# The end of the last item: second norm in two parts, a stretch without gathers, b2's products one half step later

## The chip, the cores and the metric

The kernel runs on one core of one Trainium2 chip. The metric is the device time of one execution in microseconds (us); times given for a kernel are medians over several runs, with the lowest and the highest run beside them. Engine names are those of the profile: PE is TensorE (matrix products and transposes), PEld its weight loads, DVE is VectorE, ACT is ScalarE, POOL is GpSimd, SP is the engine that issues most DMAs.

## The reference, cut to what matters

The input x is (8, 256, 32, 32) in float32: eight items, each of 1024 tokens with 256 channels. Two layers follow one another.

```
# layer 0: attention of 8 heads of 64, the softmax over the query axis, w_out, residual
a[i, j] = softmax over i of (q[i] . k[j] / 8), for each head
x[i] = x[i] + (sum over j of a[i, j] v[j], heads side by side) @ w_out + b_out

# layer 1, on t (1024 tokens x 256 channels of an item)
n1 = norm(t);  t = t + softmax(n1 W^T n1^T) n1
n2 = norm(t);  t = t + moe(n2)

def moe(n2):                              # 8 experts, each token takes its best two
    rw, re = top2(softmax(n2 @ router_w.T));  rw = rw / sum(rw)
    out = n2
    for e in range(8):
        out += gate[:, e] * (gelu(n2 @ w1[e] + b1[e]) @ w2[e] + b2[e])
    return out
```

Here norm takes the mean off each token and divides by the root of its variance plus 1e-5, and gate[:, e] is the token's weight for expert e, zero where e is not among its two. At the end t goes back to the channel-first form of x.

## The kernel before, in words

**Tiling.** Tokens lie in eight blocks of 128 (NT = 8, P = 128 partitions), channels in two halves of 128 (NCC = 2); a "half step" of the dense experts works on 512 tokens (NH2 = 2 halves) of one expert (E = 8).

**Stages.** Items 0 to 7 go one after another through layer 0 and through the attention of layer 1 (`attend`). For items 0 to 6 the second norm (`normed`), the router (`logits`, `gates`) and `dispatch` follow; `dispatch` scatters each token's normed row twice, to the rows of its two experts in DRAM, and t + n2 is stored to DRAM (`sums`). Once item 7 is through layer 0, `experts` computes the expert products on those scattered rows and leaves the results in DRAM (`y`). What then remains of items 0 to 6 is to fetch for each token its two result rows, multiply them by the gates and add them: that is class `Results`. It is spread over the last stage, which is item 7's own `attend` and `dense`.

**Results.** There are 56 units, one for each block of items 0 to 6. A unit is *sent* by two indirect DMAs on POOL (`gather`, tile yk, line L1108), into one of 8 slots, and *added* by two DVE instructions (`add`, o, L1130). When the eight units of an item are added, its two halves are *stored* (`store`): one DVE transpose (oT, L1164) and four DMAs of 128 KB on SP's queue (L1170). `tick(place, behind)` hangs these on places of item 7's work; the table PLACES says for each place how many units are added, sent and stored. The additions are issued behind the instruction `behind`; the gathers get an order dependency on it. A scheduler orders the instructions of each engine, but keeps to these dependencies and to `issue_after`.

**Item 7's end, in its order.**

- *The last mixing.* `mix(7)` transposes the probabilities (pa, L672), copies them (aT, L674) and multiplies them with n1 (py, L679, 8 products of 128x256 for a block). DVE's "mixed" instruction (t, L684) divides by the sum of the softmax and adds t. The hook `fill("last products")` stands between aT and py of block 7.
- *The norm.* `layer_norm` takes bn_stats and bn_aggr of all eight blocks (L227 on), then adds eps, takes the root on ACT, the reciprocal on DVE (L231), and writes n2 by one DVE instruction for each block (n, L233). The tile n2 uses the buffer tag "n", the same as n1, so n2's first write waits until py of block 7 has read n1.
- *To channels.* `to_channels` makes 16 transposes on PE (pt_n, L243) and two DVE copies of 128x1024 (n2T, L244), one for each half of the channels.
- *The sum.* POOL adds n2 to t (L794), one instruction of 128x2048.
- *The router.* Eight router products (pl, L706) lead to a copy on ACT (lT, L714), two transposes (plT), DVE's copy g_l (L732), the maximum, a subtraction, exp on ACT (g_p), and some twenty small DVE instructions until all_gates (L1201 to L1203).
- *The dense experts.* `dense` makes 16 half steps. `hidden` makes eight products 128x512 (pdh, L1227) and two gelu on ACT (dh, L1236); `collect` makes 16 products 128x256 (pdy, L1251) and four DVE instructions that add gate times pdy to t (L1260). The program goes `hidden(k + 1)`, `collect(k)`. Three experts' weights have a buffer each; when expert e is done, SP loads those of expert e + 3 (`weights`, L1177 and L1181).
- *The biases.* gate times b2, summed over the experts, is one more product: `biases` transposes all_gates (pg, L1209, eight times), copies them on ACT (gT, L1211), makes 16 products with b2 (pb, L1215) and has DVE add them to t (L1218). It is called between hidden(1) and collect(0):

```
for at, (e, n) in enumerate((e, n) for e in range(E) for n in range(NH2)):
    now = (e, n, hidden(e, n))
    if at == 1:
        biases()
    if pending is not None:
        collect(*pending)
    pending = now
```

After the last expert, item 7's two halves go out by the same `store`.

Of the kernel before, what the change touches and what calls it, by code (L numbers as in the profile page):

```python
# [10 lines left out]
F32 = mybir.dt.float32  # L11
I32 = mybir.dt.int32
AF = mybir.ActivationFunctionType
ALU = mybir.AluOpType
# [5 lines left out]
def kernel(  # L20
# [23 lines left out]
    nc = tc.nc  # L44
    P = 128
    B, C, S = x.shape
    E, D, FF = w1.shape
# [4 lines left out]
    NT = S // P  # L52
# [12 lines left out]
    one = ctx.enter_context(tc.tile_pool(name="one", bufs=1))  # L65
# [3 lines left out]
    small = ctx.enter_context(tc.tile_pool(name="small", bufs=6))  # L69
# [147 lines left out]
    def bcast(t, n):  # L217

        return t.unsqueeze(2).to_broadcast([P, NT, n])

    def layer_norm(t, dst, eps, name):

        mv = small.tile([P, NT, 2], F32, tag="mv", name=f"mv_{name}")
        for i in range(NT):
            st = small.tile([P, nc.vector.BN_STATS_DIM], F32, tag="st", name=f"st_{name}_{i}")
            nc.vector.bn_stats(st, t[:, i, :])
            nc.vector.bn_aggr(mv[:, i, :], st)  # L227
        rstd = small.tile([P, NT], F32, tag="rstd", name=f"rstd_{name}")
        nc.vector.tensor_scalar_add(rstd, mv[:, :, 1], eps)
        nc.scalar.activation(rstd, rstd, AF.Sqrt)  # L230
        nc.vector.reciprocal(rstd, rstd)  # L231
        for i in range(NT):
            written = nc.vector.tensor_scalar(  # L233
                dst[:, i, :], t[:, i, :], mv[:, i, 0:1], rstd[:, i : i + 1], ALU.subtract, ALU.mult
            )
        return written

    def to_channels(t, dst, name):

# [107 lines left out]
    class Begin:  # L347
# [3 lines left out]
        def __init__(self, b, xT):  # L351
            self.b, self.xT = b, xT
            self.v = None
            self.qks = [[]]
            self.todo = list(range(NT))
# [270 lines left out]
    def attend(b, t1, fill, tick=nothing):  # L626
        n1 = one.tile([P, NT, D], F32, tag="n", name=f"n1_{b}")
        layer_norm(t1, n1, 1e-5, f"a{b}")
        fill("norm 1")
        nT = one.tile([P, NCC, S], F32, tag="nT", name=f"nT_{b}")  # L630
        to_channels(n1, nT, f"n1_{b}")
        fill("normed 1")
        xa = one.tile([P, NCC, S], F32, tag="xa", name=f"xa_{b}")
        for ec in range(NCC):
            px = big(f"px_{b}_{ec}")
            for dc in range(NCC):
                for n in range(NH2):
                    nc.tensor.matmul(  # L638
                        px[:, ts(n, 512)],
                        WT[:, dc, ts(ec, P)],  # L640
                        nT[:, dc, ts(n, 512)],
                        start=(dc == 0),
                        stop=(dc == NCC - 1),
                    )
            tick(("xa", ec), nc.vector.tensor_copy(xa[:, ec, :], px))

        t2 = t1

        def scores(i):
            psc = big(f"ps1_{b}_{i}")  # L650
            for ec in range(NCC):
                for n in range(NH2):
                    nc.tensor.matmul(  # L653
                        psc[:, ts(n, 512)],
                        xa[:, ec, ts(i, P)],
                        nT[:, ec, ts(n, 512)],
                        start=(ec == 0),
                        stop=(ec == NCC - 1),
                    )
            nmax = small.tile([P, 1], F32, tag="nmax", name=f"nmax_{b}_{i}")  # L660
            tick(("max", i), nc.vector.tensor_reduce(nmax, psc, AX.X, ALU.max, negate=True))  # L661
            ex = expp.tile([P, 1024], F32, tag="exps", name=f"ex1_{b}_{i}")
            ssum = small.tile([P, 1], F32, tag="ssum", name=f"ssum_{b}_{i}")
            nc.scalar.activation(ex, psc, AF.Exp, bias=nmax, scale=1.0, accum_out=ssum)  # L664
            return ex, ssum

        def mix(i, ex, ssum):
            if i == NT - 1:
                fill("last weights")
            pt = big(f"pa_{b}_{i}")  # L670
            for m in range(NT):
                nc.tensor.transpose(pt[:, ts(m, P)], ex[:, ts(m, P)], ident)  # L672
            aT = two.tile([P, S], F32, tag="tr", name=f"aT_{b}_{i}")
            nc.vector.tensor_copy(aT, pt)  # L674
            if i == NT - 1:
                fill("last products")
            py = acc(f"py_{b}_{i}")
            for m in range(NT):
                nc.tensor.matmul(  # L679
                    py[:, :D], aT[:, ts(m, P)], n1[:, m, :], start=(m == 0), stop=(m == NT - 1)  # L680
                )
            rs = small.tile([P, 1], F32, tag="rs1", name=f"rs1_{b}_{i}")
            nc.vector.reciprocal(rs, ssum)
            mixed = nc.vector.scalar_tensor_tensor(  # L684
                t2[:, i, :], py[:, :D], rs, t1[:, i, :], ALU.mult, ALU.add
            )
            tick(("mixed", i), mixed)

        pending = None
        for i in range(NT):  # L690
            now = (i, *scores(i))
            if pending is not None:
                mix(*pending)
            pending = now
        mix(*pending)
        return t2

# [85 lines left out]

    groups = [Group(n, items) for n, items in enumerate(GROUPS)]

    def normed(b, t2, fill, tick=nothing):

        n2 = one.tile([P, NT, D], F32, tag="n", name=f"n2_{b}")
        tick("normed", layer_norm(t2, n2, 1e-5, f"f{b}"))
        fill("norm 2")  # L790
        nT = one.tile([P, NCC, S], F32, tag="nT", name=f"n2T_{b}")
        tick("turned", to_channels(n2, nT, f"n2_{b}"))

        nc.gpsimd.tensor_add(t2, t2, n2)  # L794
        fill("normed 2")
        l = logits(b, nT)
        return n2, nT, l
# [256 lines left out]
    class Results:  # L1054
# [9 lines left out]
            **{("max", i): (0, 1, 0) for i in range(1, 8)},  # L1064
            ("mixed", 0): (4, 2, 0),
            **{("mixed", i): (3, 2, 1 if i > 2 else 0) for i in range(1, 7)},
            ("mixed", 7): (0, 2, 0),
            "normed": (0, 2, 0),
            "turned": (3, 2, 0),
            "gates": (3, 2, 0),  # L1070
            ("dense", 0): (3, 2, 2),
            ("dense", 1): (3, 2, 0),
            **{("dense", k): (2, 2, 2) for k in range(2, 16)},
        }

        def __init__(self, group):
# [71 lines left out]
        def tick(self, place, behind=None):  # L1148
            added, sent, stored = self.PLACES.get(place, (0, 0, 0))
            if added:  # L1150
                with tc.issue_after(behind.ins):
                    for _ in range(added):
                        self.add()
            for _ in range(sent):
                self.gather(behind)
            for _ in range(stored):
                if self.whole:
                    b, total, n = self.whole.pop(0)
                    store(b, total, n)

    def store(b, total, n):

        oT = two.tile([P, D // SQ, P], F32, tag="qk1", name=f"oT_{b}_{n}")
        nc.vector.transpose(  # L1164
            oT.rearrange("p g (t i) -> p i g t", i=NB),
            total[:, ts(n, NB), :].rearrange("p i (g c) -> p i g c", c=SQ),
        )
        dst = out[b].rearrange("(g c) (n a k) -> n a c g k", c=SQ, n=NH2, a=NQ)
        for a in range(NQ):
            nc.sync.dma_start(dst[n, a], oT[ts(a, SQ)])  # L1170

    def dense(b, t2, tick):


        def weights(e):
# [11 lines left out]
        nc.sync.dma_start(b2_rows, b2)  # L1187
        for e in range(NWB):
            weights(e)
        _, nT, l = normed(b, t2, tick, tick)  # L1190
        routing = gates(b, l)
        while True:
            try:
# [80 lines left out]
        pending = None  # L1274
        for at, (e, n) in enumerate((e, n) for e in range(E) for n in range(NH2)):
            now = (e, n, hidden(e, n))
            if at == 1:
                biases()
            if pending is not None:
                collect(*pending)  # L1280
            pending = now
# [7 lines left out]
    for b in range(B):  # L1289
        xT = next_x  # L1290
        if b + 1 < B:
            next_x = load_x(b + 1)
        if b > 0:
            xs = load_squares(b)
        t1 = layer0(b, xT, begun, routing, xs)
        if b + 1 < B:
            begun = Begin(b + 1, next_x)
            t2 = attend(b, t1, begun.at)
            n2, _, l = normed(b, t2, begun.at)
            nc.sync.dma_start(groups[0].sums[b], t2)  # L1300
            routing = dispatch(b, n2, l, groups[0])
            continue
        experts(groups[0])
        others = Results(groups[0])
        others.begin()
        t2 = attend(b, t1, others.tick, others.tick)
        dense(b, t2, others.tick)
        assert others.added == len(others.units) and not others.whole


# [40 lines left out]
```

## Time and profile before

| what | value |
|---|---|
| time, median of 3 runs | 2412.4 us (2410.83 to 2414.67) |
| the profiled execution, its own time | 2419.8 us |
| its span in the profile | 2418.1 us |
| granted TensorE clock, mean of the span | 0.993 |
| busy: PE, PEld, DVE, ACT, POOL | 98%, 54%, 64%, 39%, 17% of the span |
| PE's last product ends | 2409.94 us |
| last store lands | 2416.79 us |
| item 7's last mixing product ends | 2272.20 us |
| item 7's all_gates are written | 2296.86 us |

The profile is of one execution, which took longer than the median of the runs; durations and positions below come from it. "Busy" counts the time in which an engine works on an instruction. A line of the timeline gives the start from the beginning of the span in us, the length from the first to the last instruction of the line in us, the engine, the source line, the operation, the output and the inputs with their shapes, the number of instructions, and in brackets the idle time ahead of it and what ended that. "remote" stands for an event that the profile does not put down to an instruction.

### The profile page before, as it was taken

The page shows a single profiled execution, that of the slowest core. Times are in us where ns is not written, and L with a number is a line of the kernel's source. Part 1 is how long each engine was busy: PE and PEld are TensorE (multiplying, and loading weights), DVE is VectorE, ACT ScalarE, POOL GpSimd, SP SyncE. Part 2 cuts the span into 40 slices and gives each one's busy share as a digit, 9 for nine tenths or more (in the row PEclk, how much of TensorE's full clock was granted, in tenths as well). Part 3 has the DMA queues.
Part 4 walks back from the last instruction along what each step waited for, and adds up shares of the span by engine and source line. Part 5 has one row for each costly group of instructions (what it writes and reads, how often), then busy time and mean ns, then how long its engine had stood idle before and what let it go on. Part 6 is the DMA issues. An engine that isn't in the chain of part 4 may idle for free.

```text
span 2418.1 us, 36817 instructions
## 1 busy us (share of the span) xinstructions
PE 2363.3 (98%) x13759; PEld 1315.7 (54%) x13759; DVE 1546.1 (64%) x3658; ACT 939.3 (39%) x1570; POOL 419.0 (17%) x391
## 2 busy tenths in 40 slices
PE   9999999999999999999999999999998999999798
PEld 3356534654466346633663366435643488886565
DVE  5774587567845785578547864786478753335865
ACT  3651366126612662166215631564145522221211
POOL 0000011001200020002000300030002144444652
PEclk9999999999999999999999999999999999999899
DMA  8993201010101010101000100000001166664553
GB/s 297 385 385 93 53 19 36 1 36 15 40 1 35 10 45 1 35 5 49 1 18 18 51 3 18 18 30 8 10 26 52 46 204 219 209 218 150 163 147 101
DMA packets 114778, 196.59 MB, mean 81 GB/s; under 512 B 15752, under 2 KB 58408, under 8 KB 112808
## 3 DMA queue, kind: packets, MB, share of 16 engines
q1 hardware_dynamic: 89592, 127.05, 16.0%
q0 software_dynamic: 25008, 67.20, 8.9%
q8 instruction: 109, 1.79, 0.3%
q14 instruction: 69, 0.57, 0.1%
HBM read 108.88 MB, written 110.90 MB: 91 GB/s over the span
## 4 chain that ended last, share of the span: by engine, by line
PE 91%; DVE 5%; ACT 2%; issue 1%; another core or an unknown queue 1%; DMA 1%; SPq 0%; DVEq 0%; ACTq 0%; POOLq 0%
PE po L528 19%; PE psc L451 18%; PE py L679 9%; PE ps L653 8%; PE pqk L333 7%; PE pr L619 5%; PE ph L1000 4%; PE pe L1025 4%; PE pv L370 4%; PE px L638 2%; PE pdy L1251 2%; PE pa L672 2%; PE pdh L1227 2%; PE pqk L311 2%; PE px L990 1%
## 5 line engine op out<-in xcount | busy, mean ns | idle before, releaser
L492 ACT ACTIVATE ex<-psc,nmax 128x1024 f32<-128x1024 f32 x512 | 570.5, 1115 | 312.3 <-DVE scrap L475 228.2
L451 PE MATMUL psc<-qk,qk 64*64 64x512 f32 x4096 | 576.6, 594 | 10.3 <-ACT ex L492 10.3
L528 PE MATMUL po<-ex,vs 64*64 64x512 f32 x4096 | 571.8, 592 | 1.5 <-DVE vs L508 0.5
L475 DVE TENSOR_SCALAR_CACHE_REDUCE scrap<-psc,nmax 128x512 f32<-128x512 f32 x512 | 384.5, 751 | 151.6 <-PE psc L451 124.6
L466 DVE TENSOR_REDUCE nmax<-psc 128x1 f32<-128x512 f32 x512 | 350.7, 685 | 9.3 <-PE psc L451 9.3
L451 PEld LDWEIGHTS psc<-qk,qk 64*64 64x64 f32 x4096 | 179.9, 132 | 287.1 <-ACT ex L492 138.9
L528 PEld LDWEIGHTS po<-ex,vs 64*64 64x64 f32 x4096 | 175.8, 132 | 275.3 <-issue 82.2
L679 PE MATMUL py<-n,aT 128*128 128x256 f32 x1024 | 239.6, 388 | 6.3 <-DVE aT L674 3.7
L653 PE MATMUL ps<-nT,xa 128*128 128x512 f32 x512 | 236.0, 592 | 0.0
L679 PEld LDWEIGHTS py<-n,aT 128*128 128x128 f32 x1024 | 192.9, 192 | 70.5 <-DVE aT L674 42.2
L863 POOL DMA_INDIRECT rows<-n,d_at x112 | 109.2, 975 | 661.7 <-DVE nmax L466 661.4
L664 ACT ACTIVATE ex<-ps,nmax 128x1024 f32<-128x1024 f32 x64 | 71.3, 1115 | 353.1 <-DVE nmax L661 320.5
L794 POOL TENSOR_TENSOR t<-t,n 128x2048 f32<-128x2048 f32 x8 | 36.2, 4531 | 919.2 <-DVE n L233 919.2
L333 PE MATMUL pqk<-xT,wqkv 128*128 128x512 f32 x384 | 171.2, 599 | 0.0
L684 DVE SCALAR_TENSOR_TENSOR t<-py,rs,t 128x256 f32<-128x256 f32 x64 | 30.8, 482 | 198.9 <-PE py L679 195.1
L653 PEld LDWEIGHTS ps<-nT,xa 128*128 128x128 f32 x512 | 93.5, 190 | 81.2 <-issue 75.1
L333 PEld LDWEIGHTS pqk<-xT,wqkv 128*128 128x128 f32 x384 | 71.0, 190 | 99.9 <-issue 77.8
L1108 POOL DMA_INDIRECT yk<-y,yat x112 | 108.9, 972 | 92.7 <-DVE t L1260 30.0
L619 PEld LDWEIGHTS pr<-wo,res 128*128 128x128 f32 x512 | 120.7, 331 | 3.7 <-ACT res L546 3.7
L370 PE MATMUL pv<-wqkv,xT 128*128 128x512 f32 x256 | 120.3, 599 | 2.0 <-ACT wqkv L106 1.1
L619 PE MATMUL pr<-wo,res 128*128 128x256 f32 x512 | 121.6, 398 | 0.3 <-ACT res L546 0.3
L298 ACT ACTIVATE qk<-pqk,b_qks 128x512 f32<-128x512 f32 x124 | 85.6, 691 | 88.9 <-PE pqk L333 79.8
(189 smaller groups left out, 2488.3 us busy)
## 6 DMA issues: line engine op xcount, KB each, us to landing
rows<-wb SPq DMA_DIRECT2D x7, 8192.0 KB
y<-yb SPq DMA_DIRECT2D x63, 256.0 KB
xs<-in_x_dram SPq DMA_DIRECT2D x64, 128.0 KB
out_dram<-oT SPq DMA_DIRECT2D x64, 128.0 KB
xT<-in_x_dram SPq DMA_DIRECT2D x7, 1024.0 KB
sums<-t SPq DMA_DIRECT2D x7, 1024.0 KB
o<-sums SPq DMA_DIRECT2D x7, 1024.0 KB
wpack<-in_L_ffn_w_dram SPq DMA_DIRECT2D x4, 1024.0 KB
```

Source lines behind the costliest of these rows:

```text
L333: mm = nc.tensor.matmul(pq[:, ts(n, 512)], wqkv[:, cc, t, ts(g, P)], xT[:, cc, ts(n, 512)], start=(cc == 0), stop=(cc == NCC - 1),)
L370: nc.tensor.matmul(pv, self.xT[:, cc, ts(i, P)], wqkv[:, cc, 2, :], start=(cc == 0), stop=(cc == NCC - 1),)
L451: mm = nc.tensor.matmul(pss[at, h][ts(c, DK), ts(n, 512)], k[r, j * P + c * DK : j * P + (c + 1) * DK], q[r, ts(n, 512)], start=True, stop ...
L466: firsts[at, h] = nc.vector.tensor_reduce(nmax, pss[at, h][:, ts(0, 512)], AX.X, ALU.max, negate=True)
L475: seconds[h] = nc.vector.tensor_scalar(scrap, pss[at, h][:, ts(1, 512)], -1.0, nmaxes[at, h], ALU.mult, ALU.min, accum_out=nmax,)
L492: nc.scalar.activation(ex, pss.pop((at, h)), AF.Exp, bias=nmaxes.pop((at, h)), scale=1.0, accum_out=sums[at][:, h : h + 1],)
L528: mm = nc.tensor.matmul(po[n][ts(h, DK), :], vss[at][keys, h, :], exps[at, h][keys, ts(n, 512)], start=(j == 0 and turn == 0), stop=(j == ...
L619: nc.tensor.matmul(pr[:, :C], own(res[:, g, :], i), wo[:, g, :], start=(g == 0), stop=(g == NPAIR - 1))
L653: nc.tensor.matmul(psc[:, ts(n, 512)], xa[:, ec, ts(i, P)], nT[:, ec, ts(n, 512)], start=(ec == 0), stop=(ec == NCC - 1),)
L679: nc.tensor.matmul(py[:, :D], aT[:, ts(m, P)], n1[:, m, :], start=(m == 0), stop=(m == NT - 1))
L863: scatter = nc.gpsimd.indirect_dma_start(out=view[:, :], out_offset=bass.IndirectOffsetOnAxis(ap=ats[k][:, i : i + 1], axis=0), in_=n2[:, ...
L1108: ins = nc.gpsimd.indirect_dma_start(out=self.slot(at)[:, k, :], out_offset=None, in_=self.group.y[:, :], in_offset=bass.IndirectOffsetOnAxis(
```

## The change

Five things are altered, all in item 7's end.

1. The norm becomes a class `Norm`, which can be worked off in parts; each part has its own statistics, eps, root, reciprocal and rows. For item 7, blocks 0 to 6 of the second norm are placed at `fill("last products")`, and DVE's last "mixed" instruction is issued after them (`issue_after`); block 7 follows in `normed`. n2 gets the buffer tag "xa" (xa has been read for the last time by then) in place of "n".
2. PLACES holds no entry any more for the last mixing, the norm and the turn to channels: up to the gates nothing is gathered, added or stored. Before, these places sent two units each, and the turn added three.
3. The units left out come later: the gates and dense 0 send three each, and the dense steps from 2 to 9 send and add three and two in turn, with one store each; sending ends at step 12 (it was spread over all steps before, two units sent and added and up to two stores each).
4. `biases` is called one half step later (at == 2).
5. The last item's eight stores alternate between the queues of SP and ACT.

```diff
+    class Norm:
+        def __init__(self, t, dst, eps, name):
+            self.t, self.dst, self.eps, self.name = t, dst, eps, name
+            self.mv = small.tile([P, NT, 2], F32, tag="mv", name=f"mv_{name}")
+            self.rstd = small.tile([P, NT], F32, tag="rstd", name=f"rstd_{name}")
+
+        def blocks(self, first, end):
+            t, mv, rstd = self.t, self.mv, self.rstd
+            for i in range(first, end):
...
+                nc.vector.bn_stats(st, t[:, i, :])
+                nc.vector.bn_aggr(mv[:, i, :], st)
+            some = rstd[:, first:end]
+            nc.vector.tensor_scalar_add(some, mv[:, first:end, 1], self.eps)
+            nc.scalar.activation(some, some, AF.Sqrt)
+            nc.vector.reciprocal(some, some)
+            for i in range(first, end):
+                written = nc.vector.tensor_scalar(
...
+            return written
+
     def layer_norm(t, dst, eps, name):
...
+        return Norm(t, dst, eps, name).blocks(0, NT)

     def attend(b, t1, fill, tick=nothing):
...
-            if i == NT - 1:
-                fill("last products")
+            ahead = fill("last products") if i == NT - 1 else None
             py = acc(f"py_{b}_{i}")
...
-            mixed = nc.vector.scalar_tensor_tensor(
-                t2[:, i, :], py[:, :D], rs, t1[:, i, :], ALU.mult, ALU.add
-            )
+            with tc.issue_after(ahead.ins) if ahead else nullcontext():
+                mixed = nc.vector.scalar_tensor_tensor(
+                    t2[:, i, :], py[:, :D], rs, t1[:, i, :], ALU.mult, ALU.add
+                )
             tick(("mixed", i), mixed)

-    def normed(b, t2, fill, tick=nothing):
-
-        n2 = one.tile([P, NT, D], F32, tag="n", name=f"n2_{b}")
-        tick("normed", layer_norm(t2, n2, 1e-5, f"f{b}"))
+    def normed(b, t2, fill, tick=nothing, norm=None):
+
+        if norm is None:
+            n2 = one.tile([P, NT, D], F32, tag="n", name=f"n2_{b}")
+            tick("normed", layer_norm(t2, n2, 1e-5, f"f{b}"))
+        else:
+            n2 = norm.dst
+            tick("normed", norm.blocks(NT - 1, NT))
         fill("norm 2")

         PLACES = {                      # place: (added, sent, stored)
...
-            ("mixed", 7): (0, 2, 0),
-            "normed": (0, 2, 0),
-            "turned": (3, 2, 0),
-            "gates": (3, 2, 0),
-            ("dense", 0): (3, 2, 2),
+            "gates": (3, 3, 0),
+            ("dense", 0): (1, 3, 2),
             ("dense", 1): (3, 2, 0),
-            **{("dense", k): (2, 2, 2) for k in range(2, 16)},
+            **{("dense", k): (3 - k % 2, 3 - k % 2, 1) for k in range(2, 10)},
+            ("dense", 10): (3, 2, 1),
+            ("dense", 11): (2, 0, 1),
+            ("dense", 12): (3, 0, 2),
+            ("dense", 13): (0, 0, 2),
         }

     def store(b, total, n):
...
         for a in range(NQ):
-            nc.sync.dma_start(dst[n, a], oT[ts(a, SQ)])
+            queue = nc.scalar if b == B - 1 and a % 2 else nc.sync
+            queue.dma_start(dst[n, a], oT[ts(a, SQ)])

-    def dense(b, t2, tick):
+    def dense(b, t2, norm, tick):
...
-        _, nT, l = normed(b, t2, tick, tick)
+        _, nT, l = normed(b, t2, tick, tick, norm)
...
-            if at == 1:
+            if at == 2:
                 biases()

-        t2 = attend(b, t1, others.tick, others.tick)
-        dense(b, t2, others.tick)
+        norm = None
+        def fill(place):
+            nonlocal norm
+            others.tick(place)
+            if place == "last products":
+                norm = Norm(t1, one.tile([P, NT, D], F32, tag="xa", name=f"n2_{b}"), 1e-5, f"f{b}")
+                return norm.blocks(0, NT - 1)
+
+        t2 = attend(b, t1, fill, others.tick)
+        dense(b, t2, norm, others.tick)
```

More of the change, by code (lines that the diff above doesn't have):

```diff
@@ L219, in bcast @@
         return t.unsqueeze(2).to_broadcast([P, NT, n])
-    def layer_norm(t, dst, eps, name):
[L223 to L234, printed above, removed]
-            )
-        return written
+    class Norm:
[6 more added lines that the diff above has]
+            for i in range(first, end):
+                st = small.tile(
+                    [P, nc.vector.BN_STATS_DIM], F32, tag="st", name=f"st_{self.name}_{i}"
+                )
[7 more added lines that the diff above has]
+                written = nc.vector.tensor_scalar(
+                    self.dst[:, i, :],
+                    t[:, i, :],
+                    mv[:, i, 0:1],
+                    rstd[:, i : i + 1],
+                    ALU.subtract,
+                    ALU.mult,
+                )
+            return written
+    def layer_norm(t, dst, eps, name):
+        return Norm(t, dst, eps, name).blocks(0, NT)
     def to_channels(t, dst, name):
@@ L683, in mix @@
             nc.vector.reciprocal(rs, ssum)
-            mixed = nc.vector.scalar_tensor_tensor(
-                t2[:, i, :], py[:, :D], rs, t1[:, i, :], ALU.mult, ALU.add
-            )
+            with tc.issue_after(ahead.ins) if ahead else nullcontext():
+                mixed = nc.vector.scalar_tensor_tensor(
+                    t2[:, i, :], py[:, :D], rs, t1[:, i, :], ALU.mult, ALU.add
+                )
             tick(("mixed", i), mixed)
```

## The prediction

> **What bounds the kernel now.** I read the page first. TensorE (PE) is busy 98% of the span and leads the chain that ended last with 91%, so only time in which PE stands still or runs at a lower clock can be won. The change touches only the last item's end, so next I read the timeline of that stretch, engine by engine, and then a table by windows for the clock.
>
> ```profile
> PE 2363.3 (98%) x13759; PEld 1315.7 (54%) x13759; DVE 1546.1 (64%) x3658; ACT 939.3 (39%) x1570; POOL 419.0 (17%) x391
> ```
>
> The timeline, from the last mixing to the first steady step of the dense experts:
>
> ```profile
> 2263.34 8.86 PE L679 MATMUL py<-n,aT 128*128 128x256 f32 x32 [2.60 <-issue]
> ...
> 2271.98 1.95 DVE L1164 STREAM_TRANSPOSE oT<-o 128x1024 f32<-128x1024 f32 x1
> 2273.78 0.41 DVE L684 SCALAR_TENSOR_TENSOR t<-py,rs,t 128x256 f32<-128x256 f32 x1
> ...
> 2275.62 2.67 DVE L233 TENSOR_SCALAR n<-t,mv_f,rstd_f 128x256 f32<-128x256 f32 x8
> 2276.18 3.93 PE L243 MATMUL pt_n<-ident,n 128*128 128x128 f32 x16 [3.98 <-DVE rstd_f L231]
> ...
> 2280.34 1.23 DVE L244 COPY n2T<-pt_n 128x1024 f32<-128x1024 f32 x1 [0.25 <-PE pt_n L243]
> ...
> 2284.86 4.52 POOL L794 TENSOR_TENSOR t<-t,n 128x2048 f32<-128x2048 f32 x1
> 2285.29 4.37 DVE L1130 SCALAR_TENSOR_TENSOR o<-yk,gate,o 128x256 f32<-128x256 f32 x1
> 2286.84 0.37 ACT L714 COPY lT<-pl 128x256 f32<-128x256 f32 x1 [11.49 <-remote]
> ...
> 2289.59 0.21 DVE L732 COPY g_l<-plT 128x64 f32<-128x64 f32 x1
> ...
> 2296.63 0.23 DVE L1203 TENSOR_TENSOR all_gates<-all_gates,second 128x64 f32<-128x64 f32 x1
> ```
>
> ```profile
> 2297.00 1.03 PE L1209 MATMUL pg<-ident,all_gates 128*8 128x128 f32 x8 [2.45 <-DVE all_gates L1203]
> ...
> 2305.57 4.72 PE L1251 MATMUL pdy<-wb,dh 128*128 128x256 f32 x13
> ```
>
> The reader is to see a serial path: PE ends its last mixing product at 2272.20; the norm (DVE) ends at 2278.29, the second n2T copy at 2281.57, the gates at 2296.86, and the biases' transposes (pg) wait for the gates. Behind the biases PE has no gap: it repeats pdh 3.43 and pdy 3.45, 6.89 a half step, and ends at 2409.94. The clock in four of these windows (columns: window, length, busy time of PE, PEld, DVE, ACT, POOL, then granted clock):
>
> ```profile
> 2274.80:2278.20 3.40, 2.02 (x9) 1.48 (x9) 3.05 (x11) 0.21 (x1) 2.69 (x3) 0.50 0.84 214
> 2278.20:2281.60 3.40, 3.36 (x18) 2.01 (x18) 2.58 (x4) 0.00 (x0) 2.49 (x4) 0.50 0.45 138
> ...
> 2302.10:2305.50 3.40, 3.40 (x8) 2.22 (x8) 1.09 (x2) 0.00 (x0) 0.00 (x0) 0.50 0.76 193
> 2305.50:2308.90 3.40, 3.40 (x9) 2.71 (x9) 0.69 (x1) 0.00 (x0) 0.00 (x0) 0.50 0.00 0
> ```
>
> PE's work after 2272.20, at the full clock: transposes 1.9 (an earlier item's 16 took 1.91), router products 1.1, plT 0.3, 16 half steps 110.2, pg 1.0, pb 3.5 (16 at 0.22). That is 118.0; it takes 137.7. So 19.7 us are lost, and the change works on those.
>
> **What the skill says.** (1) "SBUF — State Buffer", Who interferes with whom: a DVE instruction with two SBUF inputs and a GpSimd instruction that reads SBUF exclude each other for a whole instruction; one with at most one SBUF input doesn't mind. The trace agrees on both: the o addition beside POOL's t addition took 4.37 us where the group's mean in the last phase is 0.51, and in the first item both n2T copies (from PSUM) took 2.35 us beside the same addition. (2) "TensorE: Matmul & The Clock Gate", What's actually happening: the clock is halved after an idle window of about 3.4 us and given back after a busy one. The table shows 0.50 in 3.4 us windows behind idle ones. (3) "ScalarE: Activation LUTs", What ACT_TABLE_LOAD costs: 1283 ns; the trace has 1283. (4) "Trainium Kernel Development and Optimization", Key Constraints: DMAs of several queues share 16 engines, and issuing from more than one only saves issue time. Before has no DMA on ACT, so this isn't shown.
>
> **The change, part by part.**
>
> *Norm in two parts.* DVE's order is the same until the store transpose ends at 2273.93. Then come, instead of mixed 7: eps, root, reciprocal (0.7 us, as from 2274.91 to 2275.58) and seven rows of n at 0.334 (2.67/8): 2277.0. Then mixed 7, its statistics, the second root and one row: 0.45 + 0.46 + 0.22 + 0.47 + 0.24 + 0.4 = 2.2, so n2 is complete at 2279.2, **0.9 later** than before: the split adds a second root chain to DVE, which was late anyway, and mixed 7 queues behind part one. What it gives: 14 of 16 transposes are done before that (PE's order now alternates the two halves by block), so one pair remains, done at 2279.7. The two copies then run to 2282.2, against 2281.57. Net: +0.6. n2 moves to another buffer, so it needn't wait for py 7's reads of n1.
>
> *No gathers and no additions up to the gates.* POOL loses 8 gathers ahead of its t addition (1.26 us apart), which so starts at 2279.4 instead of 2284.86 and ends at 2283.9. DVE loses five additions, a transpose and the stalled addition, 8.2 us, between the copy and g_l. Router products end at 2283.0, lT 2283.5, plT 2284.2, **g_l 2284.3** (before 2289.59). ACT's exp table is now loaded directly behind lT, and g_p's subtraction, which reads two SBUF tiles, starts at 2284.8, 0.9 after POOL is done. Exp at 2285.1; from the end of exp to all_gates it took 4.3 (2292.55 to 2296.86): **all_gates 2289.7**, 7.2 earlier.
>
> *Biases a step later.* PE does pdh 0, pdh 1, pdy 0, pdh 2 first, so it has work from 2284.2 to 2296.3, and pg finds the gates 6 us old. DVE clears five additions (2.1) behind the gates and then pdy 0's results: no wait longer than about 0.3. pb's DVE additions (0.69) come free of the transpose that held them in before. From 2284.2 PE has 124 pdh at 0.43, 256 pdy at 0.2155, pg and pb: 53.3 + 55.2 + 1.0 + 3.5 = 113.0, so it ends at 2397.2 without clock losses. For these, which depend on where the windows fall, I take 2.4 us: one half-clock window (1.5) behind the norm, where PE now idles longer, and half a window (0.85) behind the 8-row pb. Bounds: 0 and 5.1 (three windows). **PE end 2399.6, 10.3 earlier.**
>
> *What is moved.* Six gathers are owed and repaid: the even dense steps send and add three units instead of two. POOL then needs 6 × 1.26 = 7.6 us in one step and 5.0 in the next, 12.6 in 13.8; a unit is added two steps after it was sent, so some 6 us of slack stay. DVE in a full step: six additions 2.5, transpose 2.05, its own four 1.76: 6.3 of 6.89. SP's queue: stores and weights change places, but every weight half is still issued four or five half steps (27 us) ahead of its use. I cost all that at nothing; without this cover each late unit would hold DVE and so pdy's banks.
>
> *Last store on two queues.* SP's four issues go from 2412.93 to 2414.76 and the last lands at 2416.79. Two of them leave the queue (0.47 each), but the engines are nearly full at the end: −0.8, bounds −1.0 and +0.5, since an issue from ACT isn't seen.
>
> Sum: −11.1 against this execution, whose own time is 2419.8 (span 2418.1 and 1.7 around it). That is 7.4 above the median of the runs, 2412.4, and it holds two pauses that the trace explains by nothing: DVE waits 3.1 and ACT 11.5 "remote", each some 3.5 us behind PE's record. Without the second, lT would come at 2283.5, and ACT would have exp's table in place at g_p, 2.0 us earlier; the gates stay bound by DVE's stalled addition. So on the median I count **−9.1: 2403.3 us**.
>
> **Rivals.** A: *the clock eats half.* PE now trickles transposes from 2275 to 2279.7; if windows up to 2291 stay at half rate and pb costs a window more (5.1 instead of 2.4), and if g_p meets POOL's addition (up to 1.5), it gives −5: 2407.5. For: six such windows in before. Against: from 2284.2 PE is packed. B, slower: *the repaid gathers become the bound.* 25 units in ten steps need 10 gathers per 13.78 us, so POOL falls behind from a pitch of 1.38 us on; measured is 1.26, with single rows at 1.57. At 1.78 the five pairs lose 20 us, less 6 of slack: +5, 2417.4. Against: the pitch held in 40 gathers of the dense steps. C: *it doesn't do what it says*: the time to the gates was covered by something else in runs without a profile, and only the tail stays: −1, 2411.4. Against it stands pg's 2.45 us wait on all_gates.
>
> **Numbers.** Main case 0.70 (its own range 2400 to 2407, from the clock's 0 to 5.1 and the tail), A 0.18, C 0.05, B 0.07. 0.2% is 4.8 us, about what a measurement of this kernel tells from no change; A falls half on either side of it. Faster 0.79, same 0.14, slower 0.07. The range goes from 2399 to 2409.5: it holds the main case and A.
>
> **What would show it.** all_gates near 2289.7 (of before's clock), g_l within 1 us of plT, no DVE instruction of 4 us; pg without a wait on the gates; no gap over 0.5 us on PE behind plT; POOL never more than a step behind; the last store's landing 3 us behind its transpose instead of 3.9. Wrong would be: gates no earlier than 2294, or DVE waiting for yk in the dense steps.

## The result, and the profile after

The changed kernel takes 2406.54 us in the median of 7 runs (2404.41 to 2408.99), the kernel before 2414.42 in the median of 7 (2410.83 to 2415.91). The ratio is 0.9973, with a 95% interval from 0.9963 to 0.9982: **6.5 us are saved, between 4.3 and 8.9**. (The ratio is estimated from all runs of both kernels; the two medians lie 7.9 us apart.) Forecast were 9.1 us less and 2403.3 us, with a range from 2399.0 to 2409.5.

The profiled execution of after has a span of 2404.6 us (its own time 2406.3). PE's busy time hardly moved, as its work is the same:

```profile
PE 2359.7 (98%) x13759; PEld 1316.5 (55%) x13759; DVE 1540.9 (64%) x3660; ACT 938.0 (39%) x1570; POOL 420.0 (17%) x391
```

The same stretch as in the prediction, from the timeline of after (start, length, engine, line, operation, count, and in brackets the idle time ahead and what ended it):

```profile
2258.61 8.86 PE L695 MATMUL py<-n,aT 128*128 128x256 f32 x32 [2.60 <-DVE aT L691]
...
2267.25 1.94 DVE L1186 STREAM_TRANSPOSE oT<-o 128x1024 f32<-128x1024 f32 x1
...
2269.73 2.35 DVE L242 TENSOR_SCALAR n<-t,mv_f,rstd_f 128x256 f32<-128x256 f32 x7
...
2270.28 3.22 PE L260 MATMUL pt_n<-ident,n 128*128 128x128 f32 x14 [2.82 <-DVE n L242]
2271.99 0.47 DVE L701 SCALAR_TENSOR_TENSOR t<-py,rs,t 128x256 f32<-128x256 f32 x1
...
2273.81 0.41 DVE L242 TENSOR_SCALAR n<-t,mv_f,rstd_f 128x256 f32<-128x256 f32 x1
...
2274.78 2.36 DVE L261 COPY n2T<-pt_n 128x1024 f32<-128x1024 f32 x2 [0.56 <-PE pt_n L260]
...
2276.06 1.08 PE L723 MATMUL pl<-n2T,rT 128*32 128x256 f32 x8 [1.10 <-DVE n2T L261]
...
2277.08 2.08 PE L1250 MATMUL pdh<-n2T,wb 128*128 128x512 f32 x2
...
2279.08 0.95 PE L723 MATMUL pl<-n2T,rT 128*32 128x256 f32 x8
...
2280.11 0.37 ACT L731 COPY lT<-pl 128x256 f32<-128x256 f32 x1 [6.54 <-PE pl L723]
```

and PE and DVE from there to the biases:

```profile
2286.46 0.23 DVE L1226 TENSOR_TENSOR all_gates<-all_gates,second 128x64 f32<-128x64 f32 x1
```

```profile
2293.18 1.04 PE L1232 MATMUL pg<-ident,all_gates 128*8 128x128 f32 x8
...
2295.87 3.90 PE L1238 MATMUL pb<-b_rows,gT 8*128 8x256 f32 x16
```

The reader is to see that pg, pb and the dense steps have no bracket any more: PE doesn't stop between the router and its last product. The gates are there 6.5 us before pg. What is left of idle time lies ahead of the router: 2.8, 0.8 and 1.1 us. Mixed 7 (L701) starts at 2271.99, 4.5 us after PE's last mixing product (2267.47): until then DVE is at the transpose of another item's output (2267.25) and at part one of the norm.

In after the last mixing product ends 4.7 us earlier than in the first profile of before, though the change alters nothing ahead of it; in other profiles below it ends between 2264.0 and 2276.8. So positions are compared **behind the last mixing product**, and W is the time from there to PE's last product, W = 118.0 (PE's work at the full clock) + gaps (idle times of PE over 0.15 us) + the rest. The rest is mainly what a lower clock costs: half of PE's busy time in stretches of half rate, an estimate from the trace, is 5.5 of the 6.2 us in the first profile of after and 3.3 of the 4.7 in the second. The tail is what follows PE's last product.

| profile | W | gaps | rest | tail | all_gates at | pg waits |
|---|---|---|---|---|---|---|
| before | 137.7 | 10.7 | 9.1 | 8.1 | 24.7 | 2.45 |
| after | 128.9 | 4.7 | 6.2 | 8.2 | 19.2 | 0 |
| after, second profile | 128.5 | 5.7 | 4.7 | 8.2 | 18.8 | 0 |

One thing is needed to read the times below: in the profiles from some chips, engines that wait for PE are let go some 3 us late, now and then, by nothing that the profile names. Such a pause behind the last mixing product lengthens W when PE comes to wait for it. So each ratio is against runs of before on the same chip, and W is compared only between profiles without pauses (before's two profiles both have some).

### The profile page after: what moved, and what is told of

The parts are those of the page before. It is cut to its first block, busy times and chain, and to the rows that moved or that the text cites. A ratio compares the mean times of both kernels' runs of the same rounds, so it can differ in the third digit from the quotient of the medians.

```text
span 2404.6 us, 36813 instructions
## 1 busy us (share of the span) xinstructions
PE 2359.7 (98%) x13759; PEld 1316.5 (55%) x13759; DVE 1540.9 (64%) x3660; ACT 938.0 (39%) x1570; POOL 420.0 (17%) x391
## 4 chain that ended last, share of the span: by engine, by line
PE 91%; DVE 5%; ACT 2%; DMA 1%; issue 1%; POOL 0%; SPq 0%; DVEq 0%; ACTq 0%; POOLq 0%
PE po L545 19%; PE psc L468 18%; PE py L695 9%; PE ps L670 7%; PE pqk L350 7%; PE pr L636 5%; PE ph L1021 4%; PE pv L387 4%; PE pe L1046 4%; PE pdh L1250 2%; PE px L655 2%; PE pdy L1274 2%; PE pa L689 2%; PE pqk L328 2%; PE px L1011 1%
## 5 line engine op out<-in xcount | busy, mean ns | idle before, releaser
L468 PEld LDWEIGHTS psc<-qk,qk 64*64 64x64 f32 x4096 | 181.0, 132 | 285.8 <-ACT ex L509 138.0
L701 DVE SCALAR_TENSOR_TENSOR t<-py,rs,t 128x256 f32<-128x256 f32 x64 | 30.9, 482 | 194.4 <-PE py L695 194.4
```

What stands on the lines that cost most here:

```text
L468: mm = nc.tensor.matmul(pss[at, h][ts(c, DK), ts(n, 512)], k[r, j * P + c * DK : j * P + (c + 1) * DK], q[r, ts(n, 512)], start=True, stop ...
```

## The experiments

**Undoing one part at a time, and one part alone.** Four of them (the old table, the biases back, the norm in one part in its first run, the later biases alone in its first run) ran on one chip, on which before takes 2421.4 us and every profile shows pauses. After itself did not run on that chip, so how far each of the four lies from after is not measured.

*The old table.* After, with PLACES as in before.

```diff
-            "gates": (3, 3, 0),
+            ("mixed", 7): (0, 2, 0),
+            "normed": (0, 2, 0),
+            "turned": (3, 2, 0),
+            "gates": (3, 2, 0),
...
```

> The changed kernel with the table PLACES of before: eight gathers, five additions, a store's transpose and a sixth addition stand again between the last mixing and the gates. W is the time from the end of the last mixing product to PE's last product: 137.7 us in the profile of before, 128.9 in that of after. Theory 1 (two covers for one wait): PE's wait for the gates goes when the gates come early or when pg comes late, and either is enough. Here pg comes late: all_gates about 24 us behind the last mixing product, pg reached at about 26, so no wait on them; W 129 to 131, time 0 to 2 us above after. Theory 2 (the gathers and additions are what cost): the gates come 5 us later, pdy 0's evictions wait for them and hold PE's banks; W 132 to 135, time 3 to 6 us above after. Theory 3 (the clock): half-clock windows decide; W anywhere from 127 to 134, with gaps as in after.

Measured: ratio 0.9982 [0.9975, 0.9988], 4.4 us under before. The gates come at 23.6 instead of 19.2, as theory 1 has it, and PE doesn't wait on them; W is 136.7, but pb waits 2.8 us on ACT's copy gT, which is let go 2.99 late by such a pause. W decides nothing here; that pg doesn't wait speaks for theory 1.

*The biases back at half step 1.*

```diff
-            if at == 2:
+            if at == 1:
                 biases()
```

> The changed kernel with the biases back at half step 1, so that pg stands between pdh 1 and pdy 0. Theory 1 (two covers for one wait): the gates are early (19.2 us behind the last mixing product in after), and PE comes to pg at about 18.9, so pg waits 0.3 to 0.6 and pb perhaps 1 more on DVE; W 129.5 to 131, time 0.5 to 2 us above after. Theory 2 (the later biases are what gains): pg and pb wait again; W 132 to 134, time 3 to 5 above after. Theory 3 (the clock): pb, with only 8 rows, then falls into windows next to the norm's idle time; two more half-clock windows, W 131 to 134 with gaps under 6 us in sum.

Measured: ratio 0.9982 [0.9973, 0.9991], 4.4 us under before. PE's timeline of this kernel:

```profile
2295.93 1.03 PE L1232 MATMUL pg<-ident,all_gates 128*8 128x128 f32 x8 [0.36 <-DVE all_gates L1226]
...
2298.62 3.96 PE L1238 MATMUL pb<-b_rows,gT 8*128 8x256 f32 x16
```

pg waits 0.36 us and pb not at all: with early gates the later biases are worth 0.4 us of PE's idle time. W (134.6) has 3.2 us of gaps at dense steps far behind, where pauses stand.

*The norm in one part.* After, without the two lines in `fill` that make part one.

```diff
-            if place == "last products":
-                norm = Norm(t1, one.tile([P, NT, D], F32, tag="xa", name=f"n2_{b}"), 1e-5, f"f{b}")
-                return norm.blocks(0, NT - 1)
```

> The changed kernel with the second norm in one part, as before, n2 back in the buffer of n1; all else as changed. Theory 1: the split is worth nothing, since DVE is late anyway: the second n2T copy comes 9.4 us behind the last mixing product (before: 9.37, after: 9.67); W 128 to 130, time within 1 us of after. Rival (the split carries a part): with all transposes behind the whole norm the copy comes at 11 or later, W 131 to 132, time 2 to 3 above after.

Measured: ratio 0.998 [0.9972, 0.9989]; W 136.1, with 3.8 us of gaps where pauses stand. It was run again:

> After with the norm in one part once more. In its first profile the gaps ahead of the dense steps were 4.4 us in sum, against 4.7 to 5.8 with the split, and pauses hid the rest. Theory 1, sharpened: the split costs, since the second root chain and the row of block 7 come on top of a DVE that is late anyway, and the transposes' trickle keeps PE half idle; W 126 to 128, time 1 to 3 us under after (5 to 6 under before is what after gave: 8 to 11 here). Rival (the split is worth nothing either way): W 128 to 129.5, time within 1 of after. Rival (the split gains): W 130 or more apart from pauses.

Measured on a chip without pauses: 2406.78 us against 2413.84, ratio 0.9968 [0.9957, 0.998]. W is 128.9, after's 128.9 and 128.5. The gaps shrink to one of 3.95 us, from 4.7 and 5.7 in sum, but the rest grows to 7.0, from 6.2 and 4.7. My sharpened theory, that the split costs 1 to 3 us, falls: here no gain and no loss of it shows.

*The later biases alone.* The kernel before, with `at == 2` and nothing else.

> The kernel before with only the biases moved to half step 2; gathers, additions, norm and stores as before. Theory 1 (two covers for one wait): pg's wait on the gates (2.45 us) and pb's (1.1) go, and perhaps a half-clock window; a pause of some 3.5 us ahead of the copy of the router's logits, if it is there, is now seen in full, since no later wait takes it in. W 131 to 134, time 3 to 6 us under before. Theory 2 (gathers and additions are what cost): pdy 0's evictions wait for the late gates instead, and PE waits there; W 135 to 138, time 0 to 2 under before.

Measured: ratio 0.9966 [0.9952, 0.9979], 8.2 us under before. The old table's version above is this one with the split and the two store queues added; its median is 5.9 us higher. What of that is pauses is not known, and no run has the split or the queues alone. Since 8.2 us was as much as the whole change had given, both ran again on one chip, one without pauses:

> The changed kernel as it is, on a chip with the runs below. Theory 1 (two covers for one wait): W, from the end of the last mixing product to PE's last product, is again 129 unless one of the pauses of some 3.4 us falls where PE waits (each adds 3 to 5); time 5 to 8 us under before. Rival (the pauses decide): their number differs from kernel to kernel, and after has fewer than before in every profile; W without them is the same for both within 3 us.

> The kernel before with only the biases a half step later, beside after on one chip. Theory 1: the later biases alone hide the gates' lateness; time within 2 us of after, W 128 to 131 apart from pauses. Theory 2 (gathers and additions are what cost): 3 us or more above after.

Measured: before 2414.03 us; after 2406.95, ratio 0.9973 [0.9961, 0.9984]; the later biases alone 2404.82, ratio **0.9958 [0.9944, 0.9971]**. W is 128.5 and 126.5. PE in the timeline of the second:

```profile
2290.28 2.86 PE L1251 MATMUL pdy<-wb,dh 128*128 128x256 f32 x12 [0.39 <-ACT dh L1236]
...
2294.69 1.04 PE L1209 MATMUL pg<-ident,all_gates 128*8 128x128 f32 x8
```

and DVE:

```profile
2282.93 4.37 DVE L1130 SCALAR_TENSOR_TENSOR o<-yk,gate,o 128x256 f32<-128x256 f32 x1
2287.21 0.21 DVE L732 COPY g_l<-plT 128x64 f32<-128x64 f32 x1
...
2292.32 0.22 DVE L1203 TENSOR_TENSOR all_gates<-all_gates,second 128x64 f32<-128x64 f32 x1
```

The stalled addition of 4.37 us is still there, the gates are late (22.5 behind the last mixing product), and PE doesn't care: it has products of half steps 0 to 2 until 2294.69.

*The new table alone.* The kernel before, with after's PLACES; norm, biases and stores as before.

> The kernel before with only the changed table PLACES: no gathers, additions or stores from the last mixing to the gates; the norm in one part, the biases at half step 1. Theory 1 (two covers for one wait, each enough): all_gates about 17 to 18.5 us behind the last mixing product instead of 24.7, PE comes to pg at about 18.5 to 19, so pg waits under 0.5; W 127 to 130 apart from pauses (the later biases alone gave 126.5), time 6 to 10 us under before. Rival (only the later biases gain): pg or pb still waits 2 us or more, W 131 to 134, time 2 to 4 under before.

Measured on the chip of the second run of the norm in one part: 2403.64 us, ratio 0.9966 [0.9954, 0.9978]. The gates come at 17.5, pg waits 0.37, W is 127.8. So theory 1 holds from both sides: the later biases alone save 10.1 us (7.0 to 13.5), the new table alone 8.2 (5.3 to 11.1), both with split and stores 6.5 (3.9 to 9.4). The intervals overlap; what they show is that the parts don't add up, and that either of the two alone saves, within the noise, no less than the whole change.

**Taking away what is left.** In after PE idles ahead of the transposes and the router, because DVE comes late to the norm. Three more edits take that away: no additions, gathers or stores at mixings 5 and 6 (they go to dense steps 10 to 14), the second n2T copy on ACT, and the first dense product behind the last router product (`routed`).

```diff
-            **{("mixed", i): (3, 2, 1 if i > 2 else 0) for i in range(1, 7)},
+            **{("mixed", i): (3, 2, 1 if i > 2 else 0) for i in range(1, 5)},
...
+            if name == f"n2_{B - 1}" and cc == 1:
+                nc.scalar.copy(dst[:, cc, :], pt)
...
-            now = (e, n, hidden(e, n))
+            with tc.issue_after(routed[0].ins) if at == 0 else nullcontext():
+                now = (e, n, hidden(e, n))
```

> After, with four more edits: no additions, gathers or stores at the mixings of blocks 5 and 6 either (they go to dense steps 10 to 14); the second half's n2T copy on ACT; the first dense product after the last router product. If what is left is DVE's queue ahead of the norm (mixed 7 waits 4.5 us for DVE in after), n2 is complete 2.3 us behind the last mixing product instead of 6.75, the copies at about 4.2 instead of 9.67, and all_gates at about 12 instead of 19.2; W 123 to 125, and the gap of 2.6 us ahead of py 6 falls to about 1.4; time 5 to 8 us under after. Rival (the clock eats it): half-clock windows come as before, W 126 to 128, time 1 to 3 under after. Rival (the owed units become a bound): gathers and additions of steps 10 to 14 hold pdy's banks; W 129 or more, with PE gaps behind step 9.

Measured beside after and the later biases: 2402.66 us, ratio 0.9958 [0.9944, 0.9971]. W is 122.9, the gates come at 12.4, n2 is complete at 2.96: as expected, to 0.7 us. Of the 6.8 us by which the gates come earlier than in after, 3.8 are gained up to n2, 1.3 between n2 and the last copy, and 1.8 between that copy and the last router product; what each edit alone is worth was not run. But the time fell by 4.3 only, since the tail grew from 8.2 to 12.2. The chain of waits at its end (start, length, what) tells why:

```profile
2389.06 2.66 DMA out_dram<-oT
...
2391.95 1.98 DVE oT L1192
```

The last transpose waits for a buffer until a store of item 6 has left it, which now stood at dense step 14. The mended version adds block 5's units in DVE's idle time behind the last aT copy and ends the stores at step 13:

```diff
+            ("mixed", 5): (0, 2, 0),
+            "copied": (3, 0, 0),
...
-            ("dense", 12): (3, 0, 1),
-            ("dense", 13): (3, 0, 1),
-            ("dense", 14): (1, 0, 2),
+            ("dense", 12): (4, 0, 0),
+            ("dense", 13): (0, 0, 2),
```

> The version with DVE free ahead of the norm, with its tail mended: there item 6's last store stood at dense step 14, so that item 7's first transpose waited behind it and the second one for a buffer (12.2 us from PE's last product to the end of the span, 8.2 in before and after). Here block 5's additions stand in DVE's idle time behind the last aT copy, and the last store at step 13. If the step is right, W 122 to 124 and 8.2 to 8.5 behind PE: 3.5 to 4.5 us under the version before it, 12 to 15 under before. Rival (the end is bound by the engines that move the stores, however early they come): the tail stays over 10. Rival (the additions in the idle time delay mixing 6 or the norm): n2 complete later than 3.5 us behind the last mixing product, W 125 or more.

Measured: **2397.66 us against 2413.84, ratio 0.9935 [0.9921, 0.9949]**, 15.7 us under before; W 122.9, tail 8.2. PE's timeline:

```profile
2259.11 7.17 PE L700 MATMUL py<-n,aT 128*128 128x256 f32 x32 [0.55 <-DVE aT L694]
2266.12 1.69 PE L260 MATMUL pt_n<-ident,n 128*128 128x128 f32 x14
2269.30 0.44 PE L260 MATMUL pt_n<-ident,n 128*128 128x128 f32 x2 [1.49 <-DVE n L242]
2270.94 1.07 PE L730 MATMUL pl<-n2T,rT 128*32 128x256 f32 x16 [1.21 <-DVE n2T L264]
```

Fourteen transposes follow the mixing without a gap, at the full clock, and the gap ahead of the last mixings is 0.55 us instead of 2.60. This version beats before, and after too, whose interval on the other chip without pauses was 0.9961 to 0.9984.

*The split where DVE is free.* The mended version, with the norm in one part.

> The version with DVE free ahead of the norm and a mended tail, but with the norm in one part. Theory 1 (the split pays only where DVE is free): mixed 7 at 0.6 behind the last mixing product, n2 complete at 4.9 to 5.3 (2.96 with the split), the copy at 6.6 (4.6), PE idle 2 us more ahead of the transposes and the router; W 124.5 to 127 with a half-clock window more, time 2 to 4 us above the version with the split. Rival (the split is worth nothing here either): W 122.5 to 124, time within 1 us.

It fell on a chip with many pauses (before 2423.4 us): ratio 0.998 [0.9972, 0.9988], W 134.4 with 5.4 us of gaps behind the gates. Up to the gates, where its profile has no pause behind the last mixing product, the positions can be read: n2 complete at 4.6 (2.96 with the split), DVE's copy at 6.4 (4.6) and ACT's at 7.5 (4.5), the start of lT at 8.2 (5.8), all_gates at 14.8 (12.4). So the split brings the router 2.4 us forward there. What of it reaches the end was not measured undisturbed.

*Before, a second profile.*

> The kernel before, unchanged, for a second profile. The first one holds two pauses. If they belong to that execution and not to the kernel, this profile shows the copy of the router's logits (lT) about 11 us behind the last mixing product instead of 14.6, g_p's exp 2 us earlier as the prediction took it, all_gates at 22.5 to 23, pg still waiting on them (the longer, 3 to 5 us, because PE comes to it earlier), and W 134 to 136 instead of 137.7. If the pause is part of before (the order of its queues), lT comes at 14 to 15 again and W is 137 to 138. The ratio to the other runs of before is 1 within 0.1%.

Measured on that same chip: ratio 1.0004 [0.9995, 1.0012]. It has pauses again, at an n2T copy and at lT (14.6); g_p's exp comes at 21.5, the gates at 26.1, pg waits 5.1 us, W is 138.0. Taken by itself this looks like the expectation's second reading, a pause that is part of before. The later biases alone speak against it: up to the gates that kernel is the same as before, and on the chip with pauses its lT started at 14.4 and its gates came at 25.7, on the one without at 10.9 and 22.5. So the pause belongs to the execution. An undisturbed profile of before is still missing; from the first one, with the gates 2.1 us earlier (24.65 less 22.51) and all behind them unchanged, I estimate W at 135.6.

## Why the prediction was right, and where its sizes were off

**The direction, the range and the main mechanism hold.** n2 was to be complete 0.9 later; it came 0.66 later (6.75 against 6.09 behind the last mixing product). The second n2T copy was to come 0.6 later; it came 0.3 later. POOL's t addition was to start at 7.2 and did at 6.9. pg was to find the gates 6 us old; they were 6.5. No DVE instruction takes 4 us any more. PE has no gap behind plT.

**The repaid gathers** cost nothing, as said. In after's dense steps all waits of DVE behind 2284 are for PE, none for yk:

```profile
DVE t L1283 <- PE pdy L1274: 29.4, 22, 4.3
DVE t L1241 <- PE pb L1238: 4.3, 4, 3.6
```

It was closer than I thought: the pitch of the gathers is 1.26 in the median but 1.37 in the mean of 48 intervals between 2300 and 2371 (one wait of 4.5 for DVE left out), next to the 1.38 from which rival B decides. Some 2.4 us of these intervals are waits of POOL for DVE; without them the mean is 1.32. (By the table the last unit is sent at dense step 10, not 12, and added at 12.)

**The gates** came 5.4 us earlier than in that profile, not 7.2 (and 3.3 earlier than the 22.5 without its pause). The step that failed is "router products end at 2283.0": that is 10.8 behind the last mixing product, and they ended at 12.6. PE's order has two dense products between the router's halves (2277.08, 2.08 us at half clock), which I had not counted. It cost nothing at pg, which had 6.5 us to spare.

**The clock** is the term that was mis-sized. I had 7.0 us of idle time ahead of the dense steps and 2.4 of clock loss, W 127.4. Measured: 4.7 and 5.7 us of gaps, 6.2 and 4.7 of rest, W 128.9 and 128.5. The windows of after show where (window, length, busy time of PE, PEld, DVE, ACT, POOL, then the granted clock):

```profile
2271.40:2274.80 3.40, 2.63 (x12) 1.98 (x10) 2.43 (x10) 0.20 (x1) 0.43 (x1) 0.50 0.42 105
2274.80:2278.20 3.40, 2.30 (x11) 0.70 (x10) 2.34 (x2) 0.00 (x0) 3.40 (x1) 0.50 0.02 5
2278.20:2284.20 6.00, 6.00 (x22) 2.24 (x21) 2.22 (x11) 3.71 (x5) 0.68 (x1) 0.87 0.00 0
```

PE's transposes and router products trickle at half rate, in this trace from 2269.5 to 2279.8, three stretches of 3.4 us; a fourth lies behind pb. In after's second profile there is one on each side, so the same kernel had 13.7 us of half rate in one execution and 6.8 in the other (before had 17.1, five stretches; a sixth lies ahead of the last mixing product). This is rival A's mechanism; the rest came out 2.3 to 3.8 us above what I had put in, the upper one beyond my bound of 5.1, and the smaller gaps gave 1.3 to 2.3 back: W is 1.1 to 1.5 longer than forecast. The Trainium skill's page "TensorE: Matmul & The Clock Gate", What's actually happening, which the prediction used, has the clock halved after an idle window and given back after a busy one. The traces agree in part: the halved clock did come behind stretches in which PE was mostly idle. But "idle" need not be the whole stretch (PE was busy for 39% of the one ahead of 2269.5), the full rate was not given back after one with 78% busy, and behind pb the clock was halved although PE had no gap: the prediction's window of before at 2305.50, too, stands behind one in which PE was busy throughout (3.40 of 3.40), though it read its half-rate windows as standing behind idle ones. In the mended version, where PE has no long gap, the stretch behind pb is the only one of half rate in W.

**The tail** was to shrink by 0.8; it is 8.1 before and 8.2 after. Two queues issue the last stores faster, but they land no sooner:

```profile
out_dram<-oT SPq DMA_DIRECT2D x4, 128.0 KB, 2.4
out_dram<-oT ACTq DMA_DIRECT2D x4, 128.0 KB, 3.5
```

The last column is the time from issue to landing; each rests on one store whose landing the profile has, SP's first and ACT's last of the final four, so it doesn't tell that one queue is slower. The last landing comes 3.9 us behind the end of the last transpose in both kernels, where the prediction had 3 for after. The DMA engines were the bound, which the prediction named and then priced too low: in the 2.5 us from 1.0 us behind that transpose they were busy for 93% before and 94% after. The five profiles of kernels with one queue have a tail of 8.12 to 8.15, the eight with two (the 12.2 above left out) 8.22 to 8.24. PE's 1.1 to 1.5 and the tail's 0.9 are 2.0 to 2.4 of the 2.6 us that are missing; what is left is far inside the noise of the saving. The 2.0 us that I took off before for its pause is borne out by the later biases alone, whose gates come 2.1 earlier without it.

**What the prediction didn't see** is that two of its parts cover the same wait. It priced the path with both and never asked what one of them alone would give, though its own numbers held the answer: with the biases a step later PE comes to pg at 2296.3, and the old gates were there at 2296.86, or at 2294.9 without the pause. So at most 0.6 us of the 7.2 was still to be waited for. In the run of the later biases alone pg came 2.1 us behind the gates. It is luck, then, that the wrong place of the gates didn't show in the time: the prediction's path went through them, while in the kernel the later biases had left 6.5 us of slack there.

Rival C, that only the tail changes, falls: the tail is what didn't.

## What to carry to other kernels

Where a wait can be removed from both sides, by an earlier producer or a later consumer, price each side alone first: the cheaper one (here one number in one line) may be all there is, and the other only moves slack about. Ask then what PE waits for next: here DVE's queue ahead of the norm. Moving its side work into DVE's own idle time and to later steps, together with a copy on ACT and a later first dense product, brought the saving from 6.5 to 15.7 us. And when side work is pushed back, see where its last piece lands; at the end of the kernel it meets the last stores.

## What the runs showed of the hardware

Pauses: in profiles on two chips (before 2421.4 and 2423.4 us) and in the first profile of before, waits on PE end some 3 us late, at times of two engines at once, while PE's records look normal. An example from the norm in one part, first run:

```profile
2350.80 3.60 PE L1250 MATMUL pdh<-n2T,wb 128*128 128x512 f32 x8
...
2356.55 1.66 DVE L1283 SCALAR_TENSOR_TENSOR t<-pdy,all_gates,t 128x256 f32<-128x256 f32 x4 [7.34 <-remote]
2356.79 1.27 ACT L1259 ACTIVATE dh<-pdh,b1T 128x512 f32<-128x512 f32 x2 [7.37 <-remote]
2357.52 1.59 PE L1274 MATMUL pdy<-wb,dh 128*128 128x256 f32 x5 [3.12 <-ACT dh L1259]
```

All of the profiles that have pauses show one between 2233 and 2237 us, and none shows an earlier one (DVE or ACT idle over 1.5 us with "remote" as its end). On two other chips (before 2414.0 and 2413.8 us) no profile of the six kernels that ran there has any. Their cause stays open.

The clock: in all 14 profiles the granted clock changes in steps of 3.41 us, and the rate of such a stretch goes with what PE did in the one before it. Counted from 160 us ahead of the last mixing product to PE's end, and without the stretches that hold pb:

| the stretch before | PE busy in it | the next stretch |
|---|---|---|
| at full rate | up to 43% | always halved |
| at full rate | 44% to 47% | both seen |
| at full rate | 48% and more | never halved |
| at half rate | up to 81% | always stays halved |
| at half rate | 83% and more | always back at full rate |

pb, whose products use 8 rows, is a case apart. With PE busy all the while at the full rate, stretches of which pb filled up to 58% were not followed by a halved one, those with 65% and more always were. The later biases alone, beside after on one chip, had 58% in each of two stretches and no half rate behind pb; after had 95% in one, and the half rate behind it is worth about 1.7 us (an estimate, half of 3.41) of the 2.0 between their W. These are counts from this case; no edit tested them.

DVE beside POOL: where a unit's addition stood beside POOL's t addition, it took 4.4 to 5.4 us (before and the later biases alone, two profiles each); in the other ten profiles no DVE instruction of item 7's end took over 3 us. With the old table, where no addition stands there, a small product of two tiles (g_p, 128x64) took 1.84 us beside it, 0.23 in after.

ACT copies 128x1024 from PSUM in 1.01 us where DVE takes 1.23, so the half handed to ACT was no slower.
